# Linear attention: M multiplied into Wo, and sig divided by its denominator ahead of the output projection

## The chip, the cores and the metric

The kernel runs on one core of one Trainium2 chip. The metric is the device time of one execution in microseconds (us). Before the change the median of three runs is 1824.76 us (1822.91 to 1825.77).

## What is computed

The reference is a two-layer model on 4 x 256 tokens of width 512, each layer an attention-like block and a feed-forward block with a residual, all in float32. The change touches the first block alone, a linear attention with a fixed memory M and normaliser z. Cut to what matters (H = 32 heads, 8 groups of G = 4, D = 128):

```python
q = (hidden_states @ Wq.T + bq).reshape(b, s, H, D)
sig_q = jax.nn.elu(q) + 1.0
q_sel = sig_q[:, :, ::G, :]                       # one head of each group: 8 heads
num = jnp.einsum('bshd,hde->bshe', q_sel, M)
den = jnp.einsum('bshd,hd->bsh', q_sel, z)[..., None] + EPS
retrieved = num / den
out_heads = jnp.repeat(retrieved, G, axis=2)
output = out_heads.reshape(b, s, H * D) @ Wo.T
```

Since each of the 8 retrieved heads is repeated four times, the four blocks of Wo that meet it can be added up once, which gives an effective Wo of 8 x 128 rows. `elu(q) + 1` is computed as `relu(q) + exp(min(q, 0))`. After this block come a mixture of LoRA experts (called f0), a state-space block with a long input projection, and a second mixture (f1).

## The kernel before, in words

The 1024 tokens are 8 tiles of 128. `x[t]` holds a tile's residual stream with tokens on partitions; `xnT` holds the normalised activations turned, features on partitions, so that they can be a matmul's operand. `layernorm(t, ...)` makes one tile of `xnT`: statistics and scaling on VectorE and ScalarE, four transposes on TensorE (L124), and one copy out of PSUM by ScalarE (L125).

The program is written for a planner: each instruction has its priority by the order in which it is written, and the planner places it on its engine's queue when, by its own costs, its operands and buffers are free. The queues themselves run strictly in order on the chip. `tc.issue_after(ins)` puts the instructions of its block behind `ins` on the same queue. SyncE (SP) and GpSimd (POOL) issue most transfers, also in order. Loads that wait for nothing are placed far ahead of their lines: in the profile SP issues the first weights of the state-space block (L647) at 8.48 us.

The attention stage has these parts:

- Loads. `load_wq(h)` (L275) loads one head's query weights, three buffers in all; head h + 3 is asked for when head h's matmuls are issued. `bq` and `mem` follow. `mem` is M with z as its 129th column.
- Wo. For each head POOL loads the four blocks (`wo_s`, L291, two buffers) and adds them into `wo[:, h, :]` (L292 to L294).
- `queries(h)`: 8 matmuls of 128x512 (L97, 16 records in the profile) into two PSUM banks of the pool with tag `mm2`, of which there are two. Then `e = min(q + b, 0)` on VectorE (L319), `sig = relu(q + b)` on ScalarE (L321), `exp(e)` on ScalarE (L322), and their sum on VectorE (L323). The result has the head's features on partitions and tokens along the row.
- `retrieve(h)`: for each token tile a matmul with the tile of `sig` as the stationary and `mem[:, h]` as the moving operand (L335); its 129 columns are the numerators and, last, the denominator, with tokens on partitions. VectorE adds 1e-6, takes the reciprocal and multiplies (L339 to L341), three token tiles at a time.
- `turn(h)`: eight transposes (L349) bring the retrieved head back to features on partitions, and ScalarE copies them into `ret[h]` (L350).
- The loop runs `queries(i)`, `retrieve(i - 1)` and `turn(i - 2)`, so that each head's VectorE and ScalarE work lies beside the next head's matmuls. For the last head nothing is left to lie beside.
- The output projection: for each token tile eight matmuls (L363) accumulate over the heads in one PSUM bank of the tag `mm1` (four banks); VectorE adds the result to `x[t]` (L366), and `layernorm(t - 1)` is written behind it.

POOL then adds f0's bias to each `x[t]` (L371), and f0 begins with the matmuls `f_psl` (L158).

## Time and profile before

| | us |
|---|---|
| median of the runs (lowest, highest) | 1824.76 (1822.91, 1825.77) |
| the profiled execution: time, and its span | 1823.95, 1822.2 |
| TensorE busy in the span | 1781.4 (98%) |
| VectorE, ScalarE, POOL busy | 1294.7, 1192.0, 712.3 |
| first query matmul | 14.76 |
| first matmul of the output projection (L363) | 95.09 |
| first matmul of f0 (L158) | 156.22 |
| last addition into `wo` (L294) ends | 64.1 |
| last `wq` load issued | 57.6 |

The span runs from the first to the last instruction; the time is the device's for the whole execution. The granted TensorE clock is full through the attention stage. A float32 matmul stands in the records as two, so that the 64 matmuls of L97 are 128 records. The rows of the chain of waits give start, length, engine, tile, line and number of records.

### The profile page before, as it was taken

How to read it: one execution, taken by the hardware profiler on the slowest of the kernel's cores; microseconds unless marked ns; L12 is line 12 of the kernel's file. 1: busy time of each engine (PE TensorE's matmuls, PEld its weight loads, DVE VectorE, ACT ScalarE, POOL GpSimd, SP SyncE). 2: the span in 40 equal slices, each digit the busy share in tenths (PEclk: the TensorE clock that was granted, in tenths of full speed). 3: DMA queues.
4: the chain of work that ended last, by engine and by line, in shares of the span. 5: the costliest groups of instructions: out<-in, count | busy, mean ns of one | idle time of the engine just before them, and what ended most of it. 6: DMA issues, size and time to landing. Idle time of an engine off the chain costs nothing.

```text
span 1822.2 us, 21347 instructions
## 1 busy us (share of the span) xinstructions
PE 1781.4 (98%) x7664; PEld 937.8 (51%) x7664; DVE 1294.7 (71%) x1470; ACT 1192.0 (65%) x2143; POOL 712.3 (39%) x689
## 2 busy tenths in 40 slices
PE   7999988999999999999999999999999999999989
PEld 4545544555555555555555455555555555555554
DVE  4524798877777778777878677868776877777662
ACT  4311249775888488757875787668776878588741
POOL 5410241344444434443345444534444444443220
PEclk9999999999999999999999999999999999999999
DMA  8100133455456555555565546555654466546831
GB/s 319 66 1 11 49 128 112 166 146 125 122 148 147 147 147 145 145 144 115 157 154 145 130 116 150 146 140 148 151 145 110 133 168 152 124 135 151 195 117 47
DMA packets 81482, 241.24 MB, mean 132 GB/s; under 512 B 9632, under 2 KB 10656, under 8 KB 72032
## 3 DMA queue, kind: packets, MB, share of 16 engines
q1 hardware_dynamic: 48912, 171.69, 27.2%
q0 software_dynamic: 31888, 67.14, 22.1%
q8 instruction: 61, 1.00, 0.2%
q10 hardware_dynamic: 576, 1.05, 0.2%
q14 instruction: 45, 0.37, 0.1%
HBM read 177.97 MB, written 61.87 MB: 132 GB/s over the span
## 4 chain that ended last, share of the span: by engine, by line
PE 87%; DVE 4%; ACT 3%; issue 2%; DMA 2%; POOL 1%; SPq 0%; DVEq 0%; POOLq 0%; ACTq 0%
PE pa L583 25%; PE ps_p L890 18%; PE pd L583 12%; PE pb L583 6%; PE ps_y L805 5%; PE ps_q L97 3%; PE ps_o L363 3%; PE ps_xt L749 3%; PE ps_y L813 2%; PE f_pso L175 2%; DVE xT L626 1%; PE f_pso L212 1%; ACT cst L782 1%; PE ps_out L1102 1%; DMA cst<-cs_d 1%
## 5 line engine op out<-in xcount | busy, mean ns | idle before, releaser
L900 POOL DMA_DIRECT2D prod_d<-prod x217 | 190.2, 909 | 584.5 <-ACT prod L899 552.1
L782 ACT ACTIVATE cst<-cst,cs 128x128 f32<-128x128 f32 x1024 | 313.1, 398 | 5.5 <-DMA cst<-cs_d 5.5
L626 DVE SCALAR_TENSOR_TENSOR xT<-raw,convw,xT 128x1020 f32<-128x1020 f32 (+2 forms) x216 | 278.1, 1289 | 4.1
L790 DVE TENSOR_TENSOR cst<-cst,gt 128x1536 f32<-128x1536 f32 x128 | 221.2, 1757 | 13.1 <-ACT cst L788 13.0
L568 POOL TENSOR_TENSOR wsum<-win 128x256 f32<-128x256 f32 x72 | 112.0, 1556 | 264.7 <-DMA win<-in_win 248.1
L823 ACT ACTIVATE xdt<-xT 128x1024 f32<-128x1024 f32 x64 | 67.7, 1058 | 194.5 <-DVE xT L821 194.5
L788 ACT ACTIVATE cst<-cst 128x1536 f32<-128x1536 f32 x128 | 189.5, 1484 | 1.0
L805 PE MATMUL ps_y<-cst,xdt 128*64 128x128 f32 x2048 | 162.5, 279 | 4.9 <-issue 3.7
L890 PE MATMUL ps_p<-xT,wout 128*128 128x512 f32 x360 | 165.0, 593 | 0.0
L606 DVE TENSOR_TENSOR raw<-pb,keep 128x512 f32<-128x512 f32 x72 | 49.6, 689 | 162.1 <-PE pb L583 159.0
L610 DVE TENSOR_TENSOR raw<-pd,keep 128x512 f32<-128x512 f32 x72 | 49.7, 690 | 153.2 <-PE pd L583 125.6
L594 ACT COPY keep<-pa 128x512 f32<-128x512 f32 x144 | 84.7, 588 | 100.9 <-PE pa L583 100.9
L583 PE MATMUL pa<-xnT,wsum 128*128 128x512 f32 x288 | 144.5, 625 | 4.5 <-ACT keep L594 4.5
L805 PEld LDWEIGHTS ps_y<-cst,xdt 128*64 128x64 f32 x2048 | 120.9, 139 | 54.5 <-issue 52.3
L899 ACT COPY prod<-ps_p 128x512 f32<-128x512 f32 x217 | 122.4, 580 | 38.7 <-PE ps_p L890 17.9
L583 PE MATMUL pa<-tok,win 128*128 128x512 f32 x288 | 135.7, 593 | 1.9 <-DVE sg L613 1.9
L583 PE MATMUL pd<-tok,wsum 128*128 128x512 f32 x288 | 136.6, 592 | 0.0
L583 PE MATMUL pa<-xnT,win 128*128 128x512 f32 x288 | 135.8, 592 | 0.6 <-DVE raw L606 0.6
L583 PE MATMUL pa<-tok,wsum 128*128 128x512 f32 x288 | 135.5, 593 | 0.7 <-POOL wsum L571 0.5
L583 PE MATMUL pd<-xnT,wsum 128*128 128x512 f32 x288 | 135.5, 592 | 0.0
L583 PE MATMUL pb<-xnT,win 128*128 128x512 f32 x288 | 135.3, 592 | 0.0
L854 POOL TENSOR_TENSOR osum<-wout,wout 128x256 f32<-128x256 f32 x30 | 103.1, 3437 | 26.0 <-DMA wout<-in_wout 25.6
(227 smaller groups left out, 3141.7 us busy)
## 6 DMA issues: line engine op xcount, KB each, us to landing
cst<-cs_d SPq DMA_DIRECT2D x64, 1536.0 KB, 7.1
prod_d<-prod POOLq DMA_DIRECT2D x217, 256.0 KB, 5.0
win<-in_win SPq DMA_DIRECT2D x144, 256.0 KB, 3.4
wout<-in_wout SPq DMA_DIRECT2D x64, 256.0 KB, 4.2
wo_s<-in_wo POOLq DMA_DIRECT2D x8, 1024.0 KB, 5.7
out<-prod_d SPq DMA_DIRECT2D x6, 512.0 KB, 8.8
wq<-in_wq SPq DMA_DIRECT2D x8, 256.0 KB, 5.3
x_d<-x SPq DMA_DIRECT2D x8, 256.0 KB, 2.0
```

The costliest lines, as they stand in the source:

```text
L568: op(v[:, 0], w[:, 1, 0:2], w[:, 1, 2:4], ALU.add)
L583: last["pe"] = nc.tensor.matmul(ps, lhsT=wt[:, k, :], rhs=tk[:, k, :], start=start and k == 0, stop=k == 1, skip_group_check=not start,)
L594: last["keep"] = nc.scalar.copy(c, ps)
L626: nc.vector.scalar_tensor_tensor(d[:, :, k:], src[:, :, : SEQ - k], convw[:, i, TAPS - 1 - k : TAPS - k], d[:, :, k:], ALU.mult, ALU.add,)
L782: nc.scalar.activation(m[:, part, c, :], m[:, part, c, :], AF.Relu, bias=cs[:, c, h : h + 1], scale=1.0)
L788: last["exp"] = nc.scalar.activation(mf[:, hh], mf[:, hh], AF.Exp, scale=-1.0)
L790: last["cst"] = nc.vector.tensor_tensor(mf[:, hh], mf[:, hh], gr.rearrange("p c l -> p (c l)"), ALU.mult)
L805: last["pe"] = nc.tensor.matmul(flat(py)[e, toks(c)], lhsT=xdt[:, c, e], rhs=m[:, hh, c, :], start=True, stop=c % 2 == 0,)
L854: op(v[:, 0], e[:, 256:], o[:, 256:], ALU.add)
L890: last["pe"] = nc.tensor.matmul(ps, lhsT=w, rhs=y, start=i == over[0], stop=i == over[-1])
L899: nc.scalar.copy(st, ps)
L900: nc.gpsimd.dma_start(out=prod_d[m][p // 2][p % 2], in_=st, accum_op=ALU.add if over[0] else ALU.bypass)
```

## The change

M moves from the tokens to the weights. `mem` is loaded turned (`M` with its second index on partitions) and without z; z is a small tile of its own. For each head one matmul multiplies M into the head's summed Wo, and ScalarE copies the product back over `wo[:, h, :]`. `sig[h]` then is the operand of the output projection itself, and `retrieve` and `turn` are gone.

The division moves ahead of the projection. The denominators have tokens along the row. `divide(g)` makes them for four heads at once: z of a head, repeated over 32 columns (`zr`), is the stationary operand, `sig` of that head the moving one, and the output goes to that head's quarter of the PSUM partitions. Two tiles of 512 tokens make eight matmuls per group. VectorE adds 1e-6 and takes the reciprocal over all 128 partitions, SP stores one row of each quarter to DRAM and loads it back repeated over all partitions (`rb`, two heads per load), and VectorE multiplies `sig` by it. Group 0 is begun behind `queries(4)`, and its multiplications are written behind `queries(7)`; group 1 is done after the products of M and Wo.

The output projection is split. Six token tiles (four in the `mm1` banks, two in one `mm2` buffer) first take heads 0 to 3, then each tile takes heads 4 to 7 and is added to `x[t]`; the last two tiles take all heads at once.

```diff
-        mem = cw.tile([P, NKV, P + 1], F32, tag="mem", name="mem")
+        z = cw.tile([P, NKV], F32, tag="z", name="z")
+        nc.sync.dma_start(out=z, in_=a["z"])
+        mem = cw.tile([P, NKV, P], F32, tag="mem", name="mem")
         nc.sync.dma_start(out=mem, in_=a["M"])
...
+        zr = cw.tile([P, NKV, 32], F32, tag="zr", name="zr")
+        nc.vector.tensor_copy(zr, bcast(z, [P, NKV, 32]))
+        sig = [cw.tile([P, NTOK], F32, tag=f"sig{h}", name=f"sig{h}") for h in range(NKV)]
...
-            nc.vector.tensor_scalar(e, flat(ps), bq[:, h : h + 1], 0.0, ALU.add, ALU.min)
-            s = act.tile([P, NTOK], F32, tag="sig", name=f"sig{h}")
+            marks["e"] = nc.vector.tensor_scalar(e, flat(ps), bq[:, h : h + 1], 0.0, ALU.add, ALU.min)
+            s = sig[h]
...
-        def retrieve(h):
...
-        def turn(h):
...
+        def divide(g):
+            ps = Both.tile([P, 2, 512], F32, "mm2", f"ps_den{g}")
+            for n in range(2):
+                for q in range(4):
+                    nc.tensor.matmul(
+                        ps[q * 32 : (q + 1) * 32, n, :],
+                        lhsT=zr[:, 4 * g + q, :],
+                        rhs=sig[4 * g + q][:, n * 512 : (n + 1) * 512],
+                        start=True,
+                        stop=True,
+                    )
+            rd = act.tile([P, 2, 512], F32, tag="sig", name=f"rd{g}")
+            rb = {}
+            for n in range(2):
+                nc.vector.tensor_scalar(rd[:, n], ps[:, n], 1e-6, None, ALU.add)
+                nc.vector.reciprocal(rd[:, n], rd[:, n])
+                rd_d = dram.tile([4, 512], F32, tag=f"rd_d{g}{n}", name=f"rd_d{g}{n}")
+                nc.sync.dma_start(out=rd_d, in_=rd[::32, n])
+                for q in range(0, 4, 2):
+                    rb[n, q] = rbp.tile([P, 2, 512], F32, tag="rb", name=f"rb{g}{n}{q}")
+                    nc.sync.dma_start(out=rb[n, q], in_=rd_d[q : q + 2, :].unsqueeze(0).to_broadcast([P, 2, 512]))
+            yield
+            with tc.issue_after(marks["e"].ins):
+                for n in range(2):
+                    for q in range(4):
+                        s = sig[4 * g + q][:, n * 512 : (n + 1) * 512]
+                        nc.vector.tensor_tensor(s, s, rb[n, q // 2 * 2][:, q % 2], ALU.mult)
+
+        for h in range(NKV):
+            queries(h)
+            if h == 4:
+                first = divide(0)
+                next(first)
+        next(first, None)
+        for h in range(NKV):
+            ps = Both.tile([P, 512], F32, "mm1", f"ps_mw{h}")
+            nc.tensor.matmul(ps, lhsT=mem[:, h, :], rhs=wo[:, h, :], start=True, stop=True)
+            nc.scalar.copy(wo[:, h, :], ps)
+        for _ in divide(1):
+            pass
+
+        outs = {}
+        def project(t, heads):
+            for h in heads:
+                nc.tensor.matmul(
+                    outs[t], lhsT=sig[h][:, toks(t)], rhs=wo[:, h, :], start=h == 0, stop=h == NKV - 1
+                )
+
+        two = Both.tile([P, 2, 512], F32, "mm2", "ps_o45")
+        for t in range(6):
+            outs[t] = two[:, t - 4, :] if t >= 4 else Both.tile([P, 512], F32, "mm1", f"ps_o{t}")
+            project(t, range(4))
         for t in range(NT):
...
+            if t < 6:
+                project(t, range(4, NKV))
+            else:
+                outs[t] = Both.tile([P, 512], F32, "mm1", f"ps_o{t}")
+                project(t, range(NKV))
+            nc.vector.tensor_tensor(x[t], outs.pop(t), x[t], ALU.add)
...
-        "M": np.concatenate([i[a + "M"], i[a + "z"][:, :, None]], 2).transpose(1, 0, 2),
+        "M": i[a + "M"].transpose(2, 0, 1),
+        "z": i[a + "z"].T,
```

More of the change, by code (lines that the diff above doesn't have):

```diff
@@ L258, in model_kernel @@
         act = c0.enter_context(tc.tile_pool(name="act0", bufs=2))
+        rbp = c0.enter_context(tc.tile_pool(name="rb0", bufs=4))
         xp = c0.enter_context(tc.tile_pool(name="x0", bufs=1))
@@ L306, in model_kernel @@
             layernorm(t, Both, xns, on_act=t % 3 != 0)
-        ret = [cw.tile([P, NTOK], F32, tag=f"ret{h}", name=f"ret{h}") for h in range(NKV)]
-        sig, rtok = {}, {}
+        zr = cw.tile([P, NKV, 32], F32, tag="zr", name="zr")
+        nc.vector.tensor_copy(zr, bcast(z, [P, NKV, 32]))
+        sig = [cw.tile([P, NTOK], F32, tag=f"sig{h}", name=f"sig{h}") for h in range(NKV)]
         def queries(h):
@@ L323, in queries @@
             nc.vector.tensor_tensor(s, s, e, ALU.add)
-            sig[h] = s
-        def retrieve(h):
-            s = sig.pop(h)
-            r = act.tile([P, NT, P], F32, tag="rtok", name=f"rtok{h}")
-            for t0 in range(0, NT, 3):
-                n = min(3, NT - t0)
-                ps = Both.tile([P, 512], F32, "mm1", f"ps_n{h}_{t0}")
-                pn = ps[:, : n * (P + 1)].rearrange("p (t e) -> p t e", e=P + 1)
-                for i in range(n):
-                    nc.tensor.matmul(
-                        pn[:, i, :], lhsT=s[:, toks(t0 + i)], rhs=mem[:, h, :], start=True, stop=True
-                    )
-                rd = small.tile([P, 3], F32, tag="rd", name=f"rd{h}_{t0}")[:, :n]
-                nc.vector.tensor_scalar(rd, pn[:, :, P], 1e-6, None, ALU.add)
-                nc.vector.reciprocal(rd, rd)
-                nc.vector.tensor_tensor(r[:, t0 : t0 + n, :], pn[:, :, :P], bcast(rd, [P, n, P]), ALU.mult)
-            rtok[h] = r
@@ L344, in turn @@
-        def turn(h):
-            r = rtok.pop(h)
-            for half in range(2):
-                ps = Both.tile([P, 512], F32, "mm1", f"ps_t{h}_{half}")
-                for i in range(4):
-                    nc.tensor.transpose(ps[:, toks(i)], r[:, half * 4 + i, :], ident)
-                nc.scalar.copy(ret[h][:, half * 512 : (half + 1) * 512], ps)
-        for i in range(NKV + 2):
-            if i < NKV:
-                queries(i)
-            if 1 <= i <= NKV:
-                retrieve(i - 1)
-            if i >= 2:
-                turn(i - 2)
@@ L360, in model_kernel @@
-        for t in range(NT):
-            ps = Both.tile([P, 512], F32, "mm1", f"ps_o{t}")
-            for h in range(NKV):
-                nc.tensor.matmul(
-                    ps, lhsT=ret[h][:, toks(t)], rhs=wo[:, h, :], start=(h == 0), stop=(h == NKV - 1)
-                )
-            nc.vector.tensor_tensor(x[t], ps, x[t], ALU.add)
+        def divide(g):
+            ps = Both.tile([P, 2, 512], F32, "mm2", f"ps_den{g}")
+            for n in range(2):
+                for q in range(4):
+                    nc.tensor.matmul(
+                        ps[q * 32 : (q + 1) * 32, n, :],
[3 more added lines that the diff above has]
+                        stop=True,
+                    )
+            rd = act.tile([P, 2, 512], F32, tag="sig", name=f"rd{g}")
[14 more added lines that the diff above has]
+                        nc.vector.tensor_tensor(s, s, rb[n, q // 2 * 2][:, q % 2], ALU.mult)
```

## The prediction

> **What bounds the kernel now.** I read the page's first part, then the chain of waits over the attention stage in order of time, then single rows. A row of the chain is start, length, engine, tile, line and records; all times are us from the start of the span.

> ```profile
> span 1822.2 us, 21347 instructions
> PE 1781.4 (98%) x7664; PEld 937.8 (51%) x7664; DVE 1294.7 (71%) x1470; ACT 1192.0 (65%) x2143; POOL 712.3 (39%) x689
> ...
> PE 87%; DVE 4%; ACT 3%; issue 2%; DMA 2%; POOL 1%; SPq 0%; DVEq 0%; POOLq 0%; ACTq 0%
> ```

> ```profile
> 31.64 6.87 PE ps_q L97 x16
> 38.51 1.78 PE ps_n L335 x16
> 40.30 0.44 PE ps_t L349 x4
> 40.73 0.86 PE ps_q L97 x2
> 41.59 0.44 PE ps_t L349 x4
> 42.03 6.01 PE ps_q L97 x14
> ...
> 86.20 1.29 DVE e L319
> ...
> 87.52 1.11 ACT sig L321
> 88.63 0.96 ACT e L322
> ...
> 89.61 1.24 DVE sig L323
> ...
> 90.98 2.02 PE ps_n L335 x16
> 93.01 0.89 PE ps_t L349 x8
> ...
> 94.03 1.06 PE ps_t L349 x8
> 95.09 13.74 PE ps_o L363 x32
> ```

> TensorE is the bound. In this stage its work stands back to back from 14.76 to 86.2 (queries, retrieval and turning alternate), then the chain goes through the last head's DVE and ACT steps, and from 95.09 it is TensorE again. So a matmul taken out here is time taken out, as long as nothing else becomes late. A float32 matmul of 512 columns is two records: 16 records in 6.87, so 0.4294 a record and 0.859 a matmul.

> **What goes.** From the first query to the first output projection: 95.09 - 14.76 = 80.33. Of that the queries need 15.10 for heads 0 and 1 (14.76 to 29.86, with the last layernorm turns among them) and 6 x 6.87 = 41.22 for the rest, 56.32 in all. The other 24.0 is what the change removes: eight retrievals of 1.78 (14.24), eight turns of 2 x 0.44 (7.04), and 2.7 of bare latency for the last head behind 86.2. With it go 24 divisions on DVE (three instructions of 0.15, 0.17 and 0.51 each, 20 us busy) and 16 PSUM copies on ACT (0.59 each); DVE and ACT idled for PE here, so these are worth nothing.

> **What comes on TensorE.** (1) M into Wo: eight matmuls of 512 columns, 8 x 0.859 = 6.87. (2) Denominators: 16 matmuls of 512 columns with 32 output rows, in two groups of eight. One after the other a group would take 6.87. How far four of them share the array is the open size. No 128x32 tile runs in the trace before; two relatives do, eight up-projections on four row quarters, and the state products on two column halves:

> ```profile
> 1801.84 0.59 PE L212 MATMUL f_pso<-f_base,xnT 128*128 128x512 f32 x1
> 1802.37 1.56 PE L222 MATMUL f_pso<-f_up,f_hT 32*128 32x512 f32 x10
> ...
> 1804.29 0.70 PE L212 MATMUL f_rest<-f_base,xnT 128*128 128x512 f32 x1
> ```

> ```profile
> 608.87 0.66 PE L805 MATMUL ps_y<-cst,xdt 128*64 128x128 f32 x8
> 609.36 0.39 PE L813 MATMUL ps_y<-cst,xdr 128*64 128x128 f32 x4
> 609.58 0.61 PE L805 MATMUL ps_y<-cst,xdt 128*64 128x128 f32 x8
> 610.01 0.39 PE L813 MATMUL ps_y<-cst,xdr 128*64 128x128 f32 x4
> 610.23 0.61 PE L805 MATMUL ps_y<-cst,xdt 128*64 128x128 f32 x8
> ```

> The first holds exactly a group's shape: 16 records of 512 columns from 1802.37 to the next full-array matmul at 1804.29, 1.92, which is 4 x 0.43 plus 0.2 for going in and out. The second shows column tiles with a moving operand each: 12 records of 128 columns per 0.65 (609.58 to 610.23), where one after the other takes 12 x 0.111 (L335: 1.78 for 16) = 1.33; two run at once in full. The bounds for a group are thus 1.92 and 6.87, with 3.4 + 0.2 = 3.6 if only two of four overlap. [...] I take 1.92, since the L222 row has both switches in it.

> **The sum.** 56.32 + 6.87 + 2 x 1.92 = 67.03 in place of 80.33: 13.3 less, if TensorE never waits. [...] The output projection keeps its 64 matmuls (54.96) and layernorm turns.

> **Does it wait?** A time table from the records: query 4 ends at 29.86 + 3 x 6.87 = 50.5, denominators of heads 0 to 3 at 52.4, query 7 at 73.0, M.Wo at 79.9, denominators of heads 4 to 7 at 81.8, projections of heads 0 to 3 for six token tiles (24 x 0.859 = 20.6) at 102.4.
> - *DVE of a group.* Add from PSUM, 0.69 (L366's size). Reciprocal: the row `L493 DVE RECIPROCAL dt_rs<-dt_rs x1` has 6.55 for 128x1024, five times an ordinary pass (1.24), so 3.28 for 512. Two of each: 7.9. Multiplications 8 x 0.69 = 5.5 (L323's 1.24 to 1.94 for twice the size bounds one at 0.62 to 0.97).
> - *SP of a group.* Two stores of 8 KB (2.0 to landing, as the x_d stores L401) and four broadcasts of 512 KB (about 4, between win's 3.4 for 256 KB and cst's 7.1 for 1536 KB). SP is in order, so the second store stands behind the first broadcasts, at an issue of 0.33 to 0.43 each. SP has nothing else: after the last wq load (57.6) its next wait in the trace before is 120 long, for the x_d stores. DMA share between 60 and 100 is 0.00 to 0.01. z is one more 4 KB load beside bq; zr a 256-column copy of about 0.3 ahead of the first e.
> - *Group 0.* DVE done with its first half at 56.4, stored 58.7, spread by 63.5; with its second half at 61.6 (behind sig4), spread by 69. Its eight multiplications stand behind e7, at 74.5: 5 us to spare. Meanwhile e5 (due 59.5) waits up to 2 us for DVE; query 7 needs its buffer only at 66.1. If that cover were gone, e7's successors would stand in line: sig7, then group 1.
> - *The last head.* e7, relu, exp and sig7 take the same 4.65 that stood bare before, plus three or four multiplications between them on DVE (2.8): sig7 is ready near 79, M.Wo ends at 79.9. Uncovered it costs 5 to 7. ACT has 2.1 of relu and exp and 8 x 0.59 copies in the 6.9, with four PSUM buffers to absorb them.
> - *Wo.* POOL finishes the last head's sum at 64.1; M.Wo starts at 73.0, so 8.9 to spare.
> - *Group 1.* From 81.8: DVE 85.8, stored 88.1, spread 93, multiplied by 95.6; second half multiplied by 99.8. TensorE has first-half work up to 102.4. Bare, the first 13.8 would eat the whole gain; covered, nothing. Behind the waiting multiplications on DVE stands only x[0]'s addition, due at 105.9.
> - *Second pass.* A token tile now has 3.43 of matmuls between its sum and its turn, formerly 6.87. Its sum and layernorm take 2.74 (102.00 to 104.74 for tile 0), 2.9 from the last matmul. The LoRA stage already runs at this pace: L175 leaves 3.43, and PE idles 0.09 per tile. So 0 to 0.6 in six tiles; I take 0.
> - *Weights.* wq loads take 7.1 at most and are issued two queries (13.7) ahead.

> **From span to time.** The profiled execution took 1823.95 with a span of 1822.2 (1.75 around it). With 13.3 less: span 1808.9, that execution 1810.65. It was 0.81 under the median 1824.76, so the median becomes 1811.5.

> **Rivals.** About 0.2% (3.65) is what a measurement of this kernel can tell from no change.
> - *The quarters share less.* Two at a time: +3.4, 1814.9. None: 2 x 4.95 = +9.9, 1821.4, no difference that can be told. For: four full-height moving streams are nowhere in the trace, L222's four have 32 rows each. Against: two full streams ran in full. 8% and 5%.
> - *A wait appears* at one of the covers: the second pass at up to 1 a tile, sig7 behind all eight multiplications (2 to 3), a slow spread of group 1 beyond its 7 to spare. 1812.5 to 1819; 13%, most of it under 1818. That the stage turns load-bound, so nothing is gained, belongs here: the loads are out of the way at 59, so I give it almost nothing.
> - *The later stages are planned worse* (other side). The order on each queue is a planner's: SP's win loads stand at 8.48, ahead of wq 3, and POOL's osum at 64, far ahead of their lines. New costs and new homes in memory can move work in the state-space stage, where DVE is 70 to 80% busy behind TensorE. Its 72 units would have to lose 0.18 each to eat 13.3, and 0.24 each to be measurably slower, 1828.4 and up. Against: that stage's TensorE, DVE and ACT steps are tied to each other by explicit order, and its loads reuse what they did before. 6% slower, 2% level.
> - *More than summed* (a later stage planned better): 4%, 1806 to 1808.5.

> The forecast itself has 62%. Its own range is 1809.5 to 1813; with the two-at-a-time case and the waits under 1818 it makes 81%: 1808.5 to 1818. Faster 62 + 8 + 13 + 4 = 87%, same 5 + 2 = 7%, slower 6%.

> **What would show it.** Right: the first f_psl starts 13.3 earlier (156.2 before, near 142.9); a group of denominators takes 1.9; M.Wo 6.9 without gaps; TensorE has no wait for DVE between query 7 and the last projection. Wrong: denominators at 3.6 or 6.9 a group; TensorE waiting for sig, rb or xn; f_psl early by 13 but the end not, which means the later stages.

## The result, and the profile after

The changed kernel takes 1812.43 us (median of six, 1810.48 to 1813.73) where the kernel before takes 1824.49 beside it: a ratio of 0.9933 with a 95% interval of 0.9920 to 0.9946. A second set of five gave 1812.36 and the same ratio. It is 12 us faster; 1811.5 was predicted, within 1808.5 to 1818.0. The profiled execution took 1810.48 with a span of 1808.8 (predicted 1808.9).

First the page's head and the line of the chain by engine, of the changed kernel:

```profile
span 1808.8 us, 21019 instructions
PE 1768.5 (98%) x7520; PEld 918.0 (51%) x7520; DVE 1305.8 (72%) x1423; ACT 1187.4 (66%) x2135; POOL 721.2 (40%) x689
...
PE 88%; DVE 5%; ACT 3%; DMA 2%; issue 2%; POOL 1%; SPq 0%; DVEq 0%; ACTq 0%; POOLq 0%
```

TensorE is the bound as before, with 12.9 less of busy time; VectorE has 11 more. Then the chain of the attention stage in order of time (start, length, engine, tile, line, records), of the changed kernel:

```profile
14.19 2.84 PE ps_q L97 x6
17.03 1.01 PE ln_ps L124 x8
18.04 31.84 PE ps_q L97 x74
49.88 1.85 PE ps_den L336 x16
51.74 1.06 PE ps_mw L368 x2
52.79 20.60 PE ps_q L97 x48
73.39 6.02 PE ps_mw L368 x14
79.41 1.85 PE ps_den L336 x16
81.27 28.52 PE ps_o L377 x66
...
117.11 3.45 PE ps_o L377 x8
...
120.58 0.70 DVE x L392
...
121.33 3.70 PE ps_o L377 x8
...
132.78 6.88 PE ps_o L377 x16
...
139.69 0.02 DVEq L392
...
143.21 1.86 PE f_psl L158 x16
```

and the end of the projection in the kernel before:

```profile
145.79 6.88 PE ps_o L363 x16
...
152.70 0.02 DVEq L366
```

From the first query at 14.19 to the last projection TensorE hands over to another engine once, at 120.56, for 0.77: token tile 5 waits there until VectorE has added token tile 4 (L392). The last head's stretch of VectorE and ScalarE steps is gone, and the eight heads' worth of L335 and L349 of the kernel before with it. The planner placed one of the eight products M.Wo (two records at 51.74) ahead of query 5. From the first query to the first projection the stage takes 81.27 - 14.19 = 67.08 in place of 80.33.

VectorE in the same stretch, of the changed kernel (start, length, engine, line; what the idle time before it waited for stands in brackets):

```profile
74.63 2.49 DVE L358 TENSOR_TENSOR sig<-sig,rb 128x512 f32<-128x512 f32 x4
...
78.17 2.50 DVE L358 TENSOR_TENSOR sig<-sig,rb 128x512 f32<-128x512 f32 x4
...
82.54 6.55 DVE L347 RECIPROCAL rd<-rd 128x512 f32<-128x512 f32 x2
91.64 2.58 DVE L358 TENSOR_TENSOR sig<-sig,rb 128x512 f32<-128x512 f32 x4 [2.55 <-DMA rb<-rd_d]
96.81 2.52 DVE L358 TENSOR_TENSOR sig<-sig,rb 128x512 f32<-128x512 f32 x4 [2.59 <-DMA rb<-rd_d]
```

Group 0's multiplications (74.63 and 78.17) follow without a wait for their broadcasts. The round trip of group 1 is about as long as it was put: the first half of `sig` is multiplied by 94.2, the second by 99.3, while TensorE has first-pass work until 101.9.

### The profile page after: what moved, and what is told of

It is laid out like the page before. It is cut to its first block, busy times and chain, and to the rows that moved or that the text cites. A ratio compares the mean times of both kernels' runs of the same rounds, so it can differ in the third digit from the quotient of the medians.

```text
span 1808.8 us, 21019 instructions
## 1 busy us (share of the span) xinstructions
PE 1768.5 (98%) x7520; PEld 918.0 (51%) x7520; DVE 1305.8 (72%) x1423; ACT 1187.4 (66%) x2135; POOL 721.2 (40%) x689
## 4 chain that ended last, share of the span: by engine, by line
PE 88%; DVE 5%; ACT 3%; DMA 2%; issue 2%; POOL 1%; SPq 0%; DVEq 0%; ACTq 0%; POOLq 0%
PE pa L609 25%; PE ps_p L916 19%; PE pd L609 12%; PE pb L609 6%; PE ps_y L831 6%; PE ps_o L377 3%; PE ps_q L97 3%; PE ps_xt L775 3%; PE ps_y L839 3%; PE f_pso L175 2%; DVE xT L652 1%; PE f_pso L212 1%; ACT cst L808 1%; PE ps_out L1128 1%; DMA cst<-cs_d 1%
## 5 line engine op out<-in xcount | busy, mean ns | idle before, releaser
L594 POOL TENSOR_TENSOR wsum<-win 128x256 f32<-128x256 f32 x72 | 116.4, 1616 | 264.1 <-DMA win<-in_win 218.6
```

Source lines behind the costliest of these rows:

```text
L594: op(v[:, 0], w[:, 1, 0:2], w[:, 1, 2:4], ALU.add)
```

## Experiments

All are edits of the changed kernel. Since executions of one kernel spread over some 3 us, small effects are read from the traces: the table has the distance from the start of the first query record to the first record of f_psl (L158 before the change) and to the first of f0's base product (L175), then the median time and its ratio to the kernel before. Starts of records are used throughout; the chain dates the hand-over up to 0.2 later.

| kernel | to f_psl | to f0 base | time | ratio (95%) |
|---|---|---|---|---|
| before | 141.30 | 148.71 | 1824.5 | |
| changed | 128.86 | 136.27 | 1812.4 | 0.9933 (0.9920 to 0.9946) |
| e1, denominators on the whole array | 138.50 | 145.91 | 1822.0 | 0.9987 (0.9980 to 0.9994) |
| e2, on halves | 132.32 | 141.41 | 1815.8 | 0.9954 (0.9939 to 0.9969) |
| e3, no first pass | 138.25 | 145.67 | 1820.7 | 0.9979 (0.9972 to 0.9986) |
| e4, first pass of two tiles | 137.09 | 145.75 | 1820.5 | 0.9981 (0.9973 to 0.9989) |
| e5, no division | 124.75 | 132.16 | 1809.7 | 0.9923 (0.9907 to 0.9938) |
| e6, no M | 125.08 | 134.09 | 1807.9 | 0.9914 (0.9900 to 0.9927) |
| e7, first pass of eight tiles | 128.31 | 137.39 | 1813.5 (one) | |
| e8, eight tiles, f_psl first | 125.12 | 132.98 | 1808.0 | 0.9912 (0.9899 to 0.9926) |

### How far the quarters share the array

```diff
-        zr = cw.tile([P, NKV, 32], F32, tag="zr", name="zr")
-        nc.vector.tensor_copy(zr, bcast(z, [P, NKV, 32]))
+        zr = cw.tile([P, NKV, P], F32, tag="zr", name="zr")
+        nc.vector.memset(zr, 0.0)
+        for q in range(4):
+            nc.vector.tensor_copy(zr[:, q::4, q * 32 : (q + 1) * 32], bcast(z[:, q::4], [P, 2, 32]))
...
-                        ps[q * 32 : (q + 1) * 32, n, :],
+                        ps[:, n, :],
...
-                        start=True,
-                        stop=True,
+                        start=q == 0,
+                        stop=q == 3,
```

> The changed kernel, with each denominator matmul on the whole array: the stationary operand has 128 columns, z in the head's quarter and zeros elsewhere, and the four heads of a group add up in one bank. Same result, same eight matmuls per group, none beside another. The stage is measured from the first query matmul to the first matmul of f0's base product (148.88 us before the change, 136.43 after). My theory (the quarters ran four at a time, 1.85 a group): a group takes 6.87, so the stage is 10.0 longer, 146.4, and the time 1822.4. Rival (the quarters give nothing, a group's cost is hidden or is set elsewhere): the stage stays at 136.4 and the time at 1812.4.

And the same on halves:

```diff
+        zr = cw.tile([P, NKV, 64], F32, tag="zr", name="zr")
+        nc.vector.memset(zr, 0.0)
+        for q in range(2):
+            nc.vector.tensor_copy(zr[:, q::2, q * 32 : (q + 1) * 32], bcast(z[:, q::2], [P, 4, 32]))
...
-                for q in range(4):
+                for q in (0, 2, 1, 3):
...
+                        ps[q // 2 * 64 : q // 2 * 64 + 64, n, :],
...
+                        start=q % 2 == 0,
+                        stop=q % 2 == 1,
```

> The changed kernel, with the denominators on two column halves instead of four quarters: 64 columns of the stationary operand, z in one half of them, two heads adding up in each half. Theory (the gain is as many fold as there are column tiles): 3.44 + 0.2 for a group instead of 1.85, so the stage is 3.6 longer, 140.0, and the time 1816.0. Rival (sharing of full-height moving streams stops at two, and the quarters were no better): the stage stays at 136.4.

The chain of e1, denominators on the whole array:

```profile
49.75 6.87 PE ps_den L338 x16
56.62 20.60 PE ps_q L97 x48
77.22 6.88 PE ps_mw L370 x16
84.10 6.87 PE ps_den L338 x16
```

and of e2, on halves:

```profile
81.67 3.58 PE ps_den L338 x16
```

Sixteen records take 6.87 one after another, 3.58 on halves and 1.85 on quarters. Up to f_psl, e1 is 9.64 and e2 3.46 behind the changed kernel (10.0 and 3.6 were expected), the times 9.6 and 3.4. So all four quarters work beside each other, also with four moving streams of full height: 6.87 / 1.85 is 3.7 times. From e1, a group on quarters costs 6.87 - 9.64 / 2 = 2.05: 1.85, and 0.2 that the following full-array matmuls begin late (the product at 51.74 takes 1.06, not 0.86). Without the quarters the change would have been worth 2.1 us (1822.0 against 1824.1 of the kernel before in the same set; 2.8 up to f_psl). e2's larger distance to f0's base product is another matter, told under the hardware.

### What the round trip costs without its cover

```diff
-        two = Both.tile([P, 2, 512], F32, "mm2", "ps_o45")
-        for t in range(6):
-            outs[t] = two[:, t - 4, :] if t >= 4 else Both.tile([P, 512], F32, "mm1", f"ps_o{t}")
-            project(t, range(4))
         for t in range(NT):
-            if t < 6:
+            if t < 0:
                 project(t, range(4, NKV))
```

> The changed kernel without the first pass of the output projection: each token tile takes heads 0 to 7 at once. Behind the denominators of group 1 TensorE then has 3.44 of work that doesn't need group 1 instead of 20.6. In the changed kernel the first multiplied half tile of head 4 is there 11.0 after the end of those denominators. Theory (the round trip of group 1 is hidden by the first pass): TensorE waits 7.6 for VectorE's multiplications, the wait of 0.8 at token tile 5 goes, the stage is 6.8 longer, 143.2, the time 1819.2. Rival (the round trip is not what the first pass hides, VectorE and SP run ahead anyway): no change.

```diff
-        two = Both.tile([P, 2, 512], F32, "mm2", "ps_o45")
-        for t in range(6):
-            outs[t] = two[:, t - 4, :] if t >= 4 else Both.tile([P, 512], F32, "mm1", f"ps_o{t}")
+        for t in range(2):
+            outs[t] = Both.tile([P, 512], F32, "mm1", f"ps_o{t}")
             project(t, range(4))
         for t in range(NT):
-            if t < 6:
+            if t < 2:
```

> The changed kernel with a first pass over two token tiles, 6.87 of cover. Theory: the wait for the multiplications is 11.0 - 6.87 = 4.1, less the 0.8 at tile 5: the stage is 3.4 longer, 139.8, the time 1815.8; so each tile of cover is worth its 3.44 until 11.0 are reached. Rival: no change, or the same as without a first pass.

Both lose more than expected, 9.4 and 8.2 up to f_psl instead of 6.8 and 3.4. As a pair they failed: in e3 the planner by itself put heads 0 to 3 of a second token tile behind those of the first (16 records, 81.31 to 88.4), so both kernels had two tiles of cover, and the worth of one tile wasn't measured. What a gap costs can be read from e4. TensorE, then VectorE, then the stretches with the clock (busy time and number of instructions of PE, PEld, DVE, ACT and POOL, then granted clock, DMA share, GB/s):

```profile
81.38 7.13 PE L377 MATMUL ps_o<-wo,sig 128*128 128x512 f32 x16
92.69 8.74 PE L377 MATMUL ps_o<-wo,sig 128*128 128x512 f32 x16 [4.18 <-DVE sig L358]
103.59 0.66 PE L124 MATMUL ln_ps<-ident,xn 128*128 128x128 f32 x4 [2.16 <-DVE xn L121]
```

```profile
97.00 1.30 DVE L358 TENSOR_TENSOR sig<-sig,rb 128x512 f32<-128x512 f32 x2 [2.48 <-DMA rb<-rd_d]
98.22 0.68 DVE L391 TENSOR_TENSOR x<-ps_o,x 128x512 f32<-128x512 f32 x1
98.81 1.28 DVE L358 TENSOR_TENSOR sig<-sig,rb 128x512 f32<-128x512 f32 x2
100.02 0.69 DVE L108 BATCH_NORM_STATS2 ln_st<-x 128x6 f32<-128x512 f32 x1
...
101.47 0.69 DVE L391 TENSOR_TENSOR x<-ps_o,x 128x512 f32<-128x512 f32 x1 [0.55 <-PE ps_o L377]
...
103.02 0.52 DVE L121 TENSOR_SCALAR xn<-x,ln_mv,ln_rs 128x512 f32<-128x512 f32 x1
```

```profile
88.00:92.50 4.50, 0.51 (x2) 0.00 (x0) 1.83 (x2) 0.00 (x0) 0.00 (x0) 1.00 0.77 232
92.50:96.00 3.50, 3.31 (x4) 1.51 (x5) 2.02 (x4) 0.00 (x0) 0.00 (x0) 0.51 0.59 146
96.00:101.00 5.00, 5.00 (x13) 2.09 (x11) 3.88 (x7) 0.05 (x1) 0.00 (x0) 1.00 0.27 110
```

The wait itself is the expected one, 4.18 (4.1). Two things follow it. The clock is halved for 3.4 behind the gap (0.51 granted from 92.5 to 96.0), and 16 records take 8.74 instead of 7.03, 1.7 more. And token tile 0's layernorm is late: from its addition (98.22) to the end of its last step (L121) it takes 5.3, in the changed kernel 2.75, because two multiplications of the second half (98.81) and the addition of tile 1 (101.47), which waits 0.55 for TensorE, stand between its steps in VectorE's order. TensorE, whose next instruction is that turn, waits another 2.16. Less the 0.8 at tile 5 that goes, that is 7.3 of the 7.8 by which e4 is behind at the end of the projection. In e3, with the same cover, the clock is halved a second time, behind the wait of 2.16 (103.36 to 106.78), and the next 16 records take 8.32 instead of 7.03; by this it is further behind than e4. So the first pass hides the round trip, as the theory has it; that a tile of cover is worth its 3.44 is wrong near the edge, where a bare gap of 4.2 cost about twice its length.

### What the division and the product with M cost

The division taken out (the output lacks it):

```diff
-        zr = cw.tile([P, NKV, 32], F32, tag="zr", name="zr")
-        nc.vector.tensor_copy(zr, bcast(z, [P, NKV, 32]))
...
-            if h == 4:
-                first = divide(0)
-                next(first)
-        next(first, None)
...
-        for _ in divide(1):
-            pass
```

> The changed kernel without the division: no denominators, no reciprocals, no stores and broadcasts, no multiplications; the output lacks the division. Theory (of the whole division only its two groups of matmuls lie on the path, all else is covered): the stage is 2 x 1.85 = 3.7 shorter, 132.7, and the time 1808.7. Rival (the 8 us of VectorE and the DRAM round trip of each group cost time as well): more than 5 shorter, 1807 or less.

It is 4.11 shorter, which is two groups of 2.05. Eight us of VectorE per group, 16 multiplications, four stores and eight broadcasts of 512 KB cost nothing beyond that. The time, 1809.7, is 2.7 under the changed kernel's, within the spread of four executions.

The product with M taken out (the output lacks it):

```diff
-        for h in range(NKV):
-            ps = Both.tile([P, 512], F32, "mm1", f"ps_mw{h}")
-            nc.tensor.matmul(ps, lhsT=mem[:, h, :], rhs=wo[:, h, :], start=True, stop=True)
-            nc.scalar.copy(wo[:, h, :], ps)
```

> The changed kernel without M: Wo goes into the projection as it is, and the output lacks the product with M. The 6.87 of M.Wo also lay beside the last head's VectorE and ScalarE steps. The planner now puts four projections of heads 0 to 3 and a part of the denominators there and splits the second group. Theory (other ready work covers the last head as well): the stage is 6.87 shorter less 1 for the split group and 0.5 of waiting, 5.4 in all, 131.0, and the time 1807. Rival (M.Wo was the cover, and without it the last head stands bare again): only some 2 shorter, 134.4 and 1810.4.

It is 3.78 shorter up to f_psl, between the two expectations. Up to f0's base product, as they count, it comes to 134.09, which is the rival's 134.4, but 1.6 of this is a halved clock (f_psl takes 8.97 in e6's chain, 7.42 in e5's), told under the hardware; the time of 1807.9 is near the theory's 1807. TensorE's waits in e6 (who waits, for whom, us in total, times, longest), and TensorE behind query 7:

```profile
PE ps_o L373 <- DVE sig L358: 1.1, 1, 1.1
PE ps_q L97 <- ACT sig L326: 0.7, 1, 0.7
```

```profile
73.80 1.06 PE L336 MATMUL ps_den<-sig,zr 128*32 128x512 f32 x6
75.94 3.67 PE L373 MATMUL ps_o<-wo,sig 128*128 128x512 f32 x8 [1.08 <-DVE sig L358]
79.54 1.90 PE L336 MATMUL ps_den<-sig,zr 128*32 128x512 f32 x10
```

The first projection waits for a multiplication that was ordered behind the minimum `e` of query 7. Of the 2.05 between the end of query 7 at 73.89 and this projection at 75.94, TensorE is idle for 1.1; in the rest it does 6 of the 16 records of group 1's denominators. The other 10 still take as long as all 16 (1.83 in e6's chain, 1.85 in the changed kernel's); an estimate of the reason is that two matmuls of head 7 follow each other on one quarter, 4 records of 0.43 or 1.72. So these 2.05 are lost all the same. And query 5 waits 0.7 for its PSUM buffer: the denominators of group 0 hold one of the two `mm2` buffers, and the other is free only when VectorE and ScalarE have read query 4, 2.5 after its end, while the denominators last 1.85. In the changed kernel the product placed at 51.74 lies over this. With some 0.2 for one more change from quarters to the whole array, these make up 2.9 of the 3.1 between the 6.87 taken out and the 3.78 gained. M.Wo did cover something, if less than the bare 4.65 of the last head, since the planner found other work for the rest.

### The wait at token tile 5, and a better version

```diff
-        two = Both.tile([P, 2, 512], F32, "mm2", "ps_o45")
-        for t in range(6):
-            outs[t] = two[:, t - 4, :] if t >= 4 else Both.tile([P, 512], F32, "mm1", f"ps_o{t}")
+        two = [Both.tile([P, 2, 512], F32, "mm2", f"ps_o{k}") for k in (46, 57)]
+        for t in range(NT):
+            outs[t] = two[t % 2][:, t // 2 - 2, :] if t >= 4 else Both.tile([P, 512], F32, "mm1", f"ps_o{t}")
             project(t, range(4))
...
-            if t < 6:
+            if t < NT:
```

> The changed kernel with all eight token tiles in the first pass, tiles 4 to 7 in two two-bank buffers in turns (4 and 6 in one, 5 and 7 in the other). In the changed kernel TensorE waits 0.8 at token tile 5 until VectorE has read tile 4, which lies in the other bank of the same buffer. Theory (that wait belongs to the shared buffer): it goes, the stage is 0.8 shorter, 135.6. Rival (the second pass is too short for the layernorm between its tiles): the waits stay or grow, since tiles 6 and 7 now have 3.44 instead of 6.87 each.

The wait goes: in e7 the turns of the second pass stand 3.87 apart (123.59, 127.46, 131.33, 135.20) with no idle time between, and the way to f_psl is 0.55 shorter. So VectorE's addition of tile 4 held back tile 5 because both lay in one two-bank buffer (e3 and e4, where each tile has a bank of its own, have no wait at tile 5 either); the layernorm fits into 3.44. The single time of e7, 1813.5, shows no gain: its trace has the halved clock behind the projection (f_psl takes 9.09).

The next kernel keeps this edit. It also puts the last layernorm of the stage behind the first four token tiles of f_psl; `lora_mixture` calls its last argument ahead of each token tile:

```diff
-        layernorm(NT - 1, Both, act)
-        for t in range(NT):
+        for t in range(NT - 1):
             nc.gpsimd.tensor_tensor(x[t], x[t], f0_bias, ALU.add)
+
+        def last_norm(t):
+            if t == 4:
+                layernorm(NT - 1, Both, act)
+                nc.gpsimd.tensor_tensor(x[NT - 1], x[NT - 1], f0_bias, ALU.add)
...
-        lora_mixture("f0", 8, 16, f0_base, f0_cat, f0_up, route_top2, Both, act, then_norm)
+        lora_mixture("f0", 8, 16, f0_base, f0_cat, f0_up, route_top2, Both, act, then_norm, last_norm)
```

> The kernel with eight tiles in the first pass, and with the last layernorm of the stage written behind the first four router and LoRA matmul groups of f0 (L158). Before and after the change TensorE stands idle for some 2.5 us there, until VectorE has the last token tile ready. Theory: 3.7 of f_psl work covers that, so the stage is 0.8 + 2.5 shorter than in the changed kernel, 133.1, and the time 1809.1, less than both kernels. Rival (the copies out of PSUM on VectorE get in the way of the last layernorm, or f_psl waits for a bank): 135.6 and 1811.6.

The chain of e8:

```profile
135.62 3.44 PE ps_o L377 x8
139.05 0.44 PE ln_ps L124 x4
139.49 3.71 PE f_psl L158 x32
143.20 0.44 PE ln_ps L124 x4
143.64 3.71 PE f_psl L158 x32
147.34 10.30 PE f_pso L175 x24
```

TensorE passes from the projection into f_psl, and the last tile's turn finds its operand ready. The stage ends 3.29 earlier than in the changed kernel, as expected, and the time is 1808.0. The changed kernel and this one once more, beside each other on one chip:

> The changed kernel once more, on one chip with the next kernel, so that the two can be set against each other. Theory: 12.4 of the stage and nothing lost later, so some 12 under the kernel before, ratio 0.9933. Behind the last layernorm of the stage the clock is halved for 3.4 us in some executions (so in the traces of e2, e4, e6 and e7, not in those of e1, e3 and e5) and then f_psl takes 9.1 instead of 7.4.

> The kernel with eight tiles in the first pass and f_psl ahead of the last layernorm, beside the changed kernel. Theory: 3.3 under it (0.6 to 0.8 of the wait at tile 5, 2.5 of the idle stretch), up to 5 in executions in which the changed kernel runs f_psl at half the clock; f_psl stays at 7.4 since TensorE has no idle stretch ahead of it. Rival: the two are within 1 of each other, and the first result of this kernel was that chip's.

The changed kernel took 1812.36 (1811.80 to 1813.13), e8's kernel 1807.11 (1805.99 to 1810.38), ratios to the kernel before 0.9933 and 0.9907 (0.9893 to 0.9920). The traces show 3.30 of the 5.2 between the medians; this profile of the changed kernel had f_psl at the full clock (7.42), so the halved clock isn't shown to be the rest.

## Why the prediction was right

- **The sum.** 24.0 out, 10.7 in, 67.03 left; the trace has 67.08. The rest of the projection then takes longer than before by 0.8 (81.27 to 139.69, 58.4, against 95.09 to 152.70, 57.6), so the stage gains 12.4 and not 13.3.
- **The denominators.** 1.92 from the row of eight matmuls on row quarters; 1.85 and 0.2 behind it measured, 2.05. This was the step with the wide bounds (1.92 to 6.87), and the nearest row was a good guide, 0.13 too low for a group: by e1 the quarters are 6.87 / 2.05 = 3.35 times as fast as one matmul after the other. What the change back to the whole array costs is the 0.2, inside this.
- **The covers.** All held. Group 1's halves were multiplied at 94.2 and 99.3 (95.6 and 99.8 in the time table), group 0's broadcasts were in before their multiplications (74.63), Wo was summed in time. e4 shows that the cover of the first pass was needed, and e5 that nothing of the division but its matmuls was left on the path.
- **The failed step.** Of the second pass it says: "So 0 to 0.6 in six tiles; I take 0." The layernorm did fit, but 0.77 were lost at tile 5 to a buffer of two banks shared by tiles 4 and 5, which the working hadn't looked at. It is the term by which the stage gained less; e7 takes it away.
- **A step right for an incomplete reason.** Only query 7's buffer was checked. Query 5's was the tight one: e6 waits 0.7 there, and the planner's placing of a product hid it here. "Uncovered it costs 5 to 7" for the last head was too high: other ready work was at hand, and e6 lost 2.05 there, of which TensorE was idle for 1.1.
- **The span.** 13.4 shorter, where the stage gives 12.4. The first query stands at 14.19, 0.57 earlier, because in that execution the first tokens' load landed at 7.31 instead of 7.88; over the twelve traces of before and after and of the edits the first query lies between 14.02 and 14.78. The other 0.4 lies behind the stage, where two traces of one kernel differ by 1.2. That the span was forecast to 0.1 is luck by these two amounts.
- **The rival of the later stages** is out: from the first matmul on the token sums (`pd`) to the end, the span has 1612.1 before and 1611.8 and 1613.0 in two traces after, and the experiments lie between 1610.5 and 1613.7.

## What to carry to other kernels

Where TensorE's work stands back to back, count matmuls in and out and look for the row with the same shape for any that shares the array; this gave the gain within 1 us. Then ask of every buffer that is read by another engine which instruction wants it next, first of all of pairs of banks in one tile and of the nearest follower, not the third. Reckon a bare gap on TensorE at more than its length: in e4 the clock and the order of VectorE's work nearly doubled a gap of 4.2.

## What the runs showed of the hardware

A gap on TensorE was followed by 3.4 us at half the clock in some of these executions, at a cost of 1.2 to 1.8 (16 records in 8.74 in place of 7.03 in e4, f_psl in 8.97 in e6 and 7.42 in e5). The stage's end has such a gap, before and after the change: from the last projection to f_psl TensorE does eight transposes in 3.5. The stretches of the changed kernel and of e2 around it (columns as above):

```profile
139.60:143.00 3.40, 0.93 (x9) 0.69 (x8) 2.28 (x5) 0.88 (x2) 0.42 (x1) 1.00 0.00 0
143.00:146.40 3.40, 3.40 (x31) 3.40 (x30) 1.09 (x6) 1.87 (x2) 0.85 (x1) 1.00 0.00 0
```

```profile
143.50:147.20 3.70, 1.23 (x11) 0.99 (x10) 2.28 (x5) 0.88 (x2) 0.64 (x1) 1.00 0.00 0
147.20:150.60 3.40, 3.40 (x17) 3.40 (x17) 0.36 (x2) 1.87 (x2) 0.63 (x1) 0.51 0.00 0
```

In the first f_psl has 31 records in 3.4, in the second 17, at a granted clock of 1.00 and 0.51. With the same gap, the traces of e2, e4, e6 and e7 have the halved stretch (8.7 to 9.1 from f_psl to f0's base product), those of before, of both profiles after, and of e1, e3 and e5 do not (7.4). It explains why e2, e6 and e7 are 1.6 further behind by the second distance of the table of experiments than by the first.

| trace, start of the stretch | TensorE busy (of 3.41) | granted clock in the next |
|---|---|---|
| e4, 89.13 (the wait of 4.18) | 0.00 | 0.50 |
| e3, 89.71 (the wait of 3.86) | 0.81 | 0.50 |
| e7, 139.68 | 0.85 | 0.50 |
| e6, 136.30 | 0.94 | 0.50 |
| e4, 147.16 | 0.94 | 0.50 |
| e2, 143.83 | 0.95 | 0.50 |
| e3, 99.95 (the wait of 2.16) | 1.25 | 0.50 |
| e5, 136.48 | 1.46 | 1.00 |
| before, 153.69 | 1.54 | 1.00 |
| after, 138.53 | 1.55 | 1.00 |
| e1, 148.01 | 1.57 | 1.00 |
| e3, 147.74 | 1.74 | 1.00 |
| the second profile after, 138.16 | 2.02 | 1.00 |

Of these stretches, those with 1.25 or less of work were followed by half the clock, and those with 1.46 or more by the full one. Later in the executions stretches between the two went both ways (e2, from 256.46: 1.44 and full; e8, from 235.02: 1.52 and half), so no border is shown, and what sets the clock isn't either. The 2.5 without work behind the projection lies whole between two points in e7 (139.68 to 142.24, in the stretch from 139.68 to 143.09, with 0.85 of work); in six of the ten traces a point cut it. That it was cut in the profiles of before and after, so that the stage's gain is read free of it (1.00 granted in both), is chance. The e8 kernel has no gap there, and its f_psl takes 2 x 3.71.

A reciprocal of 128x512 float32 on VectorE took 3.34 at most (6.55 for two), five times the 0.65 of one of the multiplications beside it (2.58 for four at 91.64).
